# Residual additions of a convolution's output: GpSimd's two additions replaced by four adding transfers

## The chip, the cores and the metric

The kernel runs on one core of one Trainium2 chip. The metric is the device time of one execution in microseconds (us), the median over runs. A core has five engines with instruction streams of their own: TensorE (PE in the profile), which multiplies matrices into PSUM; VectorE (DVE) and ScalarE (ACT), which work elementwise; GpSimd (POOL), and SyncE (SP), which here does nothing but issue transfers (DMA). They meet through semaphores. SBUF is the on-chip memory of 128 partitions.

## The reference

The input is 16 images of 128 channels and 32 x 32 positions, in float32. First comes a self-attention with four heads over the 1024 positions of each image and a residual. Its output, here x1, goes into a quantized residual block:

```python
identity = x
out = act_quant(x)
out = conv3x3(out, weight_quant(w1))
out = batchnorm(out, gamma1, beta1)
out = act_quant(out)
out = conv3x3(out, weight_quant(w2))
out = batchnorm(out, gamma2, beta2)
return out + identity
```

`batchnorm` takes a channel's mean and variance over all images and positions, so nothing of a channel can be normalised before its convolution is done for all 16 images. `act_quant` clips to 0..1 and rounds to 15 steps; the weights are rounded to 7 steps on each side. The last line is the residual addition that this case is about: 16 images of 128 x 1024 numbers.

## The kernel before

**Attention** fills most of the time, up to about 1905 us: TensorE computes scores and weighted sums, ScalarE the exponentials, VectorE combinations of them. In it, sums over blocks of exponentials are kept in tiles `es`: SP sends the first block there (L603), and GpSimd sends the other three with a transfer that adds into the tile (L605, `accum_op`), 189 times in all. The attention's output x1 is stored in DRAM and the first convolution is woven into the attention; its outputs come back from DRAM into tiles `back` (the last image stays in a tile `y`).

**The second convolution** works in three parts by output channels (`LANED`): part 0 has 64 channels, parts 1 and 2 have 32 each. A tile of part 0 puts two images side by side on the 128 partitions, a tile of parts 1 and 2 four images. So part 0 has 8 tiles and parts 1 and 2 have 4 each (`TILES`). For each tile, `convolve` runs nine taps as matmuls for each half of the rows into PSUM (`psd`, L1252); ScalarE copies the result into SBUF (L1263), over an image of the first convolution's output that is no longer needed; VectorE takes statistics of it (BATCH_NORM_STATS2, L1274). In the last tile of a part the statistics are taken from PSUM itself, in three pieces (L1261), after an aggregate of the earlier ones (L1242). `parameters` then makes a scale and a bias out of them (L1237 spreads them over the partitions, L335 to L349 compute), through VectorE and ScalarE in turns. In part 2 a small matmul (`together`, L1312) takes the place of the spreading.

**The order.** Part 0's convolutions come first. Then, for each tile of part 1, TensorE convolves it while two tiles of part 0 are finished; then part 2 is convolved while part 1 is finished; then part 2 is finished with nothing else to do. A scheduler orders each engine's instructions within this; every engine works through its stream in order.

**Finishing a tile** (`finish`): ScalarE scales the tile in place (L1290), an engine adds the residual tile `res` to it in place (L1292), and SP sends it to the output (L1296). The 16 residual tiles (`x1` in the code) have been loaded from DRAM by SP (L1190), each into a tile of its own. The engine is VectorE, but GpSimd for tiles 2 and 5 of part 0 (`BY_POOL`). A GpSimd tile's send is held back and issued behind that of the next VectorE tile. The flag for a general path, which isn't taken here, is written by VectorE after the last addition of part 0 (L1334), and each engine loads it (L1529).

Of the kernel before, what the change touches and what calls it, by code (L numbers as in the profile page):

```python
# [12 lines left out]
ALU = mybir.AluOpType  # L13
# [181 lines left out]
def fast_path(  # L195
# [17 lines left out]
    P = 128  # L213
# [936 lines left out]
    with ExitStack() as ph:  # L1150
# [31 lines left out]
        x1 = {}  # L1182
        laned = lambda v: [v.rearrange("b (c k) n -> k (b c) n", k=step)[lo] for lo, step, _ in LANED]
        x1h, outh = laned(x1d), laned(out)
# [81 lines left out]
        def convolve(part, p):  # L1266
            last = p == TILES[part] - 1
            ends = (0, RPH, H - 8, H) if last else (0, 8, RPH, H) if not part and p == 0 else (0, RPH, H)
            for i, (r0, r1) in enumerate(zip(ends, ends[1:])):
                pair_conv(part, p, r0, r1 - r0, i if last else None)  # L1270
            if not last:
                for hf in range(NHF):
                    with nullcontext() if part else following("DVE"):
                        nc.vector.bn_stats(place2(part, p, hf), results[part, p][:, ts(hf, HALF)])  # L1274
            if p == TILES[part] - 2:
                gather2(part)

        BY_POOL = (2, 5)
        sent = []

        def finish(part, p, scale, bias, ends=(0, N)):
            y = results[part, p]
            for lo, hi in zip(ends, ends[1:]):
                some = y[:, lo:hi]
                if part == 2 and p == 0 and hi <= N // 2:
                    nc.vector.tensor_scalar(some, some, scale, bias, ALU.mult, ALU.add)
                elif len(ends) > 2 and p == 0:
                    nc.scalar.activation(some, some, AF.Identity, bias=bias, scale=scale)
                elif lo == 0:
                    nc.scalar.activation(y, y, AF.Identity, bias=bias, scale=scale)  # L1290
                engine = nc.gpsimd if not part and p in BY_POOL else nc.vector
                added = engine.tensor_tensor(some, some, x1[part, p][:, lo:hi], ALU.add)  # L1292
                sent.append((outh[part][ts(p, P), lo:hi], some))
                if part or p not in BY_POOL:
                    for to, what in reversed(sent):
                        nc.sync.dma_start(out=to, in_=what)  # L1296
                    sent.clear()
            return added

        def parameters(part):  # L1300
            if part < 2:
                spread(part, 0, OWN)
                return bn_params(1, late2[part], gb2[part])
            apart = statp.tile([P, STEPS[part], OWN], F32, name="apart")
            nc.vector.tensor_tensor(
                apart,
                late2[part][:, 0:OWN].unsqueeze(1).to_broadcast([P, STEPS[part], OWN]),
                own_lane.unsqueeze(2).to_broadcast([P, STEPS[part], OWN]),
                ALU.mult,
            )  # L1310
            together = ps_c.tile([P, STEPS[part] * OWN], F32, tag="c", name="together")
            nc.tensor.matmul(  # L1312
                together, lhsT=quad, rhs=apart.rearrange("p s k -> p (s k)"), start=True, stop=True
            )
            return bn_params(1, together, gb2[part])
# [12 lines left out]
        scale2, bias2 = parameters(0)  # L1328
        for p in range(TILES[1]):
            convolve(1, p)  # L1330
            for q in (2 * p, 2 * p + 1):
                added = finish(0, q, scale2, bias2)
        with tc.issue_after(added.ins):
            nc.vector.tensor_copy(flag, worst[0:1, :])  # L1334
        scale2, bias2 = parameters(1)
        for p in range(TILES[2]):
            convolve(2, p)
            finish(1, p, scale2, bias2)
        scale2, bias2 = parameters(2)
        parts = ((0, N // 4, N // 2, N), (0, N // 2, N), (0, N // 2, N), (0, N // 2, N))  # L1340
        for p in range(TILES[2]):
            finish(2, p, scale2, bias2, parts[p])
# [108 lines left out]
def attention_then_quantized_convs(  # L1451
# [50 lines left out]
    def conv_weights(n, wp, behind):  # L1502
# [19 lines left out]

    flag = const.tile([1, 1], mybir.dt.int32, name="flag")
    fast_path(
        nc, tc, x, xturned, wqk, wvo, bo, bnp, x1d, y1d, out, bo_sb, bnp_sb, quad, wq, sc, flag, conv_weights,
        constants,
# [94 lines left out]
```

## Time and profile before

Three runs took 1997.57, 1997.59 and 1999.94 us; the median is 1997.59.

| what | before |
|---|---|
| profiled execution, its own time | 1997.92 us |
| its span, first to last instruction | 1996.1 us |
| TensorE busy | 1975.1 us, 99% of the span |
| VectorE busy | 1528.0 us, 77% |
| ScalarE busy | 1173.3 us, 59% |
| GpSimd busy | 173.4 us, 9% |
| GpSimd's transfers (software_dynamic) | 99.10 MB, 26.2% of the 16 DMA engines' span |
| SP's transfers (hardware_dynamic) | 83.18 MB, 11.0% |

"Busy" is time in instructions; for TensorE their ends are modelled, so it isn't TensorE at its peak. A line of a timeline shows the start, the time, the engine, the kernel's line, the operation, out<-in by the program's names, shapes and the count; in brackets stands the time for which the engine was idle before it and what ended that. The chain that ended last is followed back from the last instruction, at each step to what released it.

### The profile page before, as it was taken

The numbers are of one execution on the slowest core, as the hardware profiler recorded it, in microseconds if no ns is written. First come the engines' busy times: TensorE is split into PE (matmuls) and PEld (weight loads), VectorE is DVE, ScalarE is ACT, GpSimd is POOL, SyncE is SP. The second block draws the span as 40 slices with busy tenths as digits, with TensorE's granted clock in tenths as the row PEclk, the third lists the DMA queues.
The fourth block names the chain that finished last, engine by engine and source line by source line (L and its number), as shares of the span: only waits on it lengthen the run. The fifth ranks groups of instructions, "written<-read, shape, count | busy, mean of one in ns | idle before, by whom it ended". The sixth has DMA issues, their size and how long they took to land.

```text
span 1996.1 us, 27602 instructions
## 1 busy us (share of the span) xinstructions
PE 1975.1 (99%) x10401; PEld 997.9 (50%) x10401; DVE 1528.0 (77%) x2746; ACT 1173.3 (59%) x2028; POOL 173.4 (9%) x215
## 2 busy tenths in 40 slices
PE   9999999999999999999999999999999999999996
PEld 4455544545444454544545454454545445455564
DVE  5886869778687876869777686977868697686887
ACT  4556556565655656555565655655565565556565
POOL 1110010000010010000001001000000100000000
PEclk9999999999999999999999999999999999999998
DMA  4333433334343343334334333343334343333184
GB/s 123 84 86 90 101 68 102 85 85 103 76 102 80 96 95 85 94 67 110 80 95 95 85 95 74 99 91 85 96 86 105 64 105 86 85 93 81 43 332 177
DMA packets 56351, 193.91 MB, mean 97 GB/s; under 512 B 6416, under 2 KB 6800, under 8 KB 56208
## 3 DMA queue, kind: packets, MB, share of 16 engines
q0 software_dynamic: 27216, 99.10, 26.2%
q1 hardware_dynamic: 25872, 83.18, 11.0%
q10 hardware_dynamic: 3120, 9.77, 1.5%
q8 instruction: 83, 1.36, 0.3%
q14 instruction: 60, 0.49, 0.1%
HBM read 35.27 MB, written 24.64 MB: 30 GB/s over the span
## 4 chain that ended last, share of the span: by engine, by line
PE 97%; DVE 2%; ACT 1%; issue 0%; DMA 0%; SPq 0%; DVEq 0%; ACTq 0%
PE pss L413 44%; PE psa L413 38%; PE psu L413 6%; PE pso L413 5%; PE psw L413 2%; PE psd L1252 1%; ACT back L1290 0%; DVE back L1292 0%; DVE early L1274 0%; DMA x<-in_x_dram 0%; PE psv L413 0%; DVE late L1261 0%; ACT steps L1217 0%; PE ps_a L413 0%; ACT rt L338 0%
## 5 line engine op out<-in xcount | busy, mean ns | idle before, releaser
L413 PE MATMUL pss<-u,x 128*64 128x512 f32 (+1 forms) x4128 | 1032.4, 589 | 0.0
L413 PE MATMUL psa<-e,xt 128*64 128x512 f32 x3472 | 897.9, 592 | 0.0
L595 ACT ACTIVATE e<-pss 128x512 f32<-128x512 f32 x1008 | 590.4, 596 | 442.3 <-PE pss L413 436.0
L413 PEld LDWEIGHTS pss<-u,x 128*64 128x64 f32 x4128 | 437.4, 137 | 436.2 <-issue 400.1
L413 PEld LDWEIGHTS psa<-e,xt 128*64 128x64 f32 x3472 | 379.0, 137 | 372.0 <-issue 352.4
L580 DVE TENSOR_TENSOR e<-e 128x512 f32<-128x512 f32 x252 | 171.9, 682 | 298.2 <-ACT e L595 297.8
L581 DVE TENSOR_TENSOR e<-e 128x1024 f32<-128x1024 f32 x252 | 307.6, 1221 | 10.7 <-ACT e L595 9.3
L605 POOL DMA_DIRECT2D es<-e x189 | 163.1, 863 | 1679.2 <-DVE e L584 1401.6
L413 PE MATMUL psu<-x,at_sb 128*64 128x512 f32 x512 | 183.5, 592 | 0.4 <-DMA x<-in_x_dram 0.4
L584 DVE TENSOR_TENSOR e<-e 128x512 f32<-128x512 f32 x252 | 173.0, 686 | 11.3 <-DVE e L581 0.9
L635 ACT COPY ev<-psa 128x512 f32<-128x512 f32 x189 | 99.2, 593 | 63.2 <-PE psa L413 61.8
L413 PE MATMUL pso<-z,wb_sb 128*64 128x512 f32 (+1 forms) x480 | 132.2, 539 | 0.0
L544 ACT ACTIVATE u<-psu,au_sb 128x512 f32<-128x512 f32 x127 | 87.3, 687 | 8.9 <-PE psu L413 6.1
L413 PEld LDWEIGHTS psu<-x,at_sb 128*64 128x64 f32 x512 | 61.2, 137 | 56.1 <-issue 55.5
L671 DVE TRANSPOSE_TENSOR_REDUCE part<-es 128x32 f32<-128x1024 f32 (+1 forms) x65 | 79.4, 1221 | 9.5 <-DMA es<-e 9.5
L711 DVE STREAM_TRANSPOSE rb<-sums 128x1024 f32<-128x1024 f32 (+1 forms) x66 | 79.8, 1210 | 1.6
L731 DVE TENSOR_TENSOR z<-av,rb 128x512 f32<-128x512 f32 x120 | 78.2, 683 | 0.0
L413 PEld LDWEIGHTS pso<-z,wb_sb 128*64 128x64 f32 x480 | 53.1, 137 | 44.5 <-issue 40.8
L802 DVE TENSOR_TENSOR y<-sa,s 64x512 f32<-64x512 f32 x15 | 10.3, 684 | 66.4 <-ACT sa L786 66.4
L1252 PE MATMUL psd<-padf,wq 128*32 128x512 bf16 (+3 forms) x792 | 60.0, 358 | 0.4 <-DVE padf L1204 0.4
L661 ACT COPY ev<-y 64x512 f32<-64x512 f32 x63 | 38.8, 616 | 33.2 <-DVE y L658 32.0
L413 PE MATMUL psw<-rows,filters 128*64 128x256 bf16 x540 | 57.5, 277 | 0.0
(199 smaller groups left out, 1354.4 us busy)
## 6 DMA issues: line engine op xcount, KB each, us to landing
es<-e POOLq DMA_DIRECT2D x189, 512.0 KB, 4.5
es<-e SPq DMA_DIRECT2D x63, 512.0 KB, 2.9
xt<-in_xturned_dram SPq DMA_DIRECT2D x32, 256.0 KB, 3.1
x_dram<-acc SPq DMA_DIRECT2D x16, 512.0 KB, 2.9
res<-x_dram SPq DMA_DIRECT2D x16, 512.0 KB, 10.3
x<-in_x_dram ACTq DMA_DIRECT2D x15, 512.0 KB, 3.9
y_dram<-y SPq DMA_DIRECT2D x15, 512.0 KB, 2.6
out_dram<-back SPq DMA_DIRECT2D x12, 512.0 KB, 3.7
```

Of the source, the lines that this page charges most:

```text
L413: done = nc.tensor.matmul(out_, lhsT=lhsT, rhs=rhs, start=start, stop=stop)
L544: copied = nc.scalar.activation(dst, ps, AF.Identity, bias=au_sb[:, h : h + 1])
L580: nc.vector.tensor_tensor(e[:, T3], e[:, B12], e[:, B22], ALU.add)
L581: nc.vector.tensor_tensor(e[:, T1 : T2 + 1 : T2 - T1], e[:, B12 : B11 + 1], e[:, B11 : T3 + 1 : T3 - B11], ALU.subtract)
L584: return nc.vector.tensor_tensor(e[:, T4], e[:, T2], e[:, B21], ALU.add)
L595: exps[:] = [nc.scalar.activation(e[:, 2 * c + 1 - m], ps, AF.Exp).ins]
L605: nc.gpsimd.dma_start(out=sides[g], in_=mine, accum_op=ALU.add)
L635: nc.scalar.copy(evs[g][i], psa[g][i])
L671: nc.vector.tensor_reduce(part, total.rearrange("p (k c) -> p k c", c=Q), AX.X, ALU.add, apply_transpose=True,)
L711: nc.vector.transpose(rb, rinv.unsqueeze(2).to_broadcast([P, n, Q]))
L731: nc.vector.tensor_tensor(z[:, 2 * (h % 2) + 1 - m], av[:, ts(m, HALF)], rb[:, ts(m, HALF)], ALU.mult)
L1252: nc.tensor.matmul(ps[lane], lhsT=wq[1][:, tap, LANED[part][2]], rhs=pads2[STEPS[part] * p + i][:, r0 + dy : r0 + dy + n_rows, dx : dx + W ...
```

## The change

In part 0, tiles 1, 3, 5 and 7 are no longer added by an engine. Once ScalarE has scaled such a tile, GpSimd issues a transfer from it that adds into the residual's tile, and SP sends the residual's tile to the output. VectorE adds tiles 0, 2, 4 and 6; GpSimd adds none itself. The sends of the adding tiles wait in a list: each is issued by SP behind the send of the next VectorE tile of part 0, and the last one ahead of whatever part 1 sends first. In the compiled order SP sends tiles 0, 2, 1, 4, 3, 6, 5, 7 of part 0 (before: 0, 1, 3, 2, 4, 6, 5, 7), then loads the flag, then sends part 1's.

```diff
-        BY_POOL = (2, 5)
-        sent = []
+        BY_DMA = [(0, p) for p in (1, 3, 5, 7)]
+        waiting, added = [], []
 
         def finish(part, p, scale, bias, ends=(0, N)):
...
-                engine = nc.gpsimd if not part and p in BY_POOL else nc.vector
-                added = engine.tensor_tensor(some, some, x1[part, p][:, lo:hi], ALU.add)
-                sent.append((outh[part][ts(p, P), lo:hi], some))
-                if part or p not in BY_POOL:
-                    for to, what in reversed(sent):
-                        nc.sync.dma_start(out=to, in_=what)
-                    sent.clear()
-            return added
+                to = outh[part][ts(p, P), lo:hi]
+                if (part, p) in BY_DMA:
+                    nc.gpsimd.dma_start(out=x1[part, p], in_=y, accum_op=ALU.add)
+                    waiting.append((to, x1[part, p]))
+                    continue
+                added[:] = [nc.vector.tensor_tensor(some, some, x1[part, p][:, lo:hi], ALU.add)]
+                sends = [(to, some)]
+                sends = waiting + sends if part else sends + waiting
+                waiting.clear()
+                for to, what in sends:
+                    nc.sync.dma_start(out=to, in_=what)
...
             for q in (2 * p, 2 * p + 1):
-                added = finish(0, q, scale2, bias2)
-        with tc.issue_after(added.ins):
+                finish(0, q, scale2, bias2)
+        with tc.issue_after(added[0].ins):
```

## The prediction

> **What bounds the kernel now.** I read the page's engine totals first. They name TensorE at 99% of a span of 1996.1 us, but that is an average, and the edit touches only the second convolution's output stage, from about 1948 us on. So I asked for the timelines of the engines there. VectorE, from the first residual addition (columns: start, us, engine, line, operation, out<-in, shape, count):
>
> ```profile
> 1949.32 1.22 DVE L1292 TENSOR_TENSOR back<-back,res 128x1024 f32<-128x1024 f32 x1 [1.31 <-ACT back L1290]
> ...
> 1953.68 2.45 DVE L1292 TENSOR_TENSOR back<-back,res 128x1024 f32<-128x1024 f32 x1 [0.81 <-ACT back L1290]
> 1956.06 0.68 DVE L1274 BATCH_NORM_STATS2 early<-back 128x6 f32<-128x512 f32 x1
> 1956.66 3.30 DVE L1292 TENSOR_TENSOR back<-back,res 128x1024 f32<-128x1024 f32 x1
> ...
> 1960.49 2.34 DVE L1292 TENSOR_TENSOR back<-back,res 128x1024 f32<-128x1024 f32 x2
> ```
>
> One addition takes 1.22 us, but two take 2.45 and 3.30. GpSimd's timeline shows what runs beside those two:
>
> ```profile
> 1952.66 2.39 POOL L1292 TENSOR_TENSOR back<-back,res 128x1024 f32<-128x1024 f32 x1 [42.40 <-ACT back L1290]
> 1956.48 2.40 POOL L1292 TENSOR_TENSOR back<-back,res 128x1024 f32<-128x1024 f32 x1 [1.43 <-ACT back L1290]
> ```
>
> GpSimd's additions end at 1955.05 and 1958.88; VectorE's end at 1956.13 and 1959.96, 1.08 after each. VectorE stood still while GpSimd added: 2.45 - 1.22 + 3.30 - 1.22 = 3.3 us lost. Then the chain that ended last, from 1960 to 1981:
>
> ```profile
> 1960.56 2.26 DVE back L1292 x2
> ...
> 1964.61 1.28 DVE late L1261 x3
> ...
> 1976.07 2.39 DVE early L1274 x4
> ...
> 1978.99 1.28 DVE late L1261 x3
> ```
>
> It is VectorE's without a wait for TensorE: part 1's last statistics end at 1965.89, part 2's at 1980.27. TensorE's timeline says when they could have been made:
>
> ```profile
> 1964.82 12.18 PE L1252 MATMUL psd<-padf,wq 128*32 128x512 bf16 x252
> 1980.76 0.42 PE L1312 MATMUL together<-apart,quad 128*128 128x84 f32 x2 [3.77 <-DVE apart L1305]
> ```
>
> The last convolution ends at 1976.99 (1980.76 - 3.77), and TensorE has run without a gap since 1934.68. The images that part 2 reads first (tile pad) are read again from 1960.85, so part 1's convolution ends about 1961.05. VectorE is late by 4.4 us after part 1 (1965.9 against 1961.05 and one 0.43 us statistic) and by 2.8 us after part 2. After that comes a tail with no convolution in it: parameters, the last additions, stores.
>
> **What the skill says.** The Trainium skill's "SBUF — State Buffer", section "Who interferes with whom", says that a VectorE instruction with two SBUF inputs and a GpSimd instruction that reads SBUF exclude each other. The trace agrees: 2.45 and 3.30 us instead of 1.22. The same section infers that such a VectorE addition doesn't collide with the writing of transfer descriptors by GpSimd. The trace agrees again: the attention phase issues 189 adding transfers from GpSimd (L605), among 252 VectorE additions of L581, which took 1180 to 1228 ns. "DMA: Bandwidth & Descriptors", section "SWDGE vs HWDGE vs iDMA", says that adding during a transfer is possible from GpSimd's queue alone; the trace has these, in just this size and type:
>
> ```profile
> L605 POOL DMA_DIRECT2D es<-e x189: 852/859/1172, 21.4 to 1866.9; - x189
> DMA to landing us min/median/max: 4.5/4.5/6.6
> ```
>
> **The change part by part.** The compiled order of the changed kernel has TensorE's and ScalarE's streams as before; VectorE loses two additions, GpSimd swaps two additions for four transfers, SP's sends change order and waits.
>
> 1. *GpSimd's two additions go* (tiles 2 and 5). Their 4.8 us were on GpSimd, off the chain; what they gave VectorE's chain is the 3.3 us above.
> 2. *VectorE does tiles 0, 2, 4, 6 instead of 0, 1, 3, 4, 6, 7*: two fewer, 1.14 us each back to back (1949.32 to 1950.46), so 2.3 us. With the first item VectorE has 5.6 us less work before part 1's statistics.
> 3. *Who is late next there?* ScalarE. It scales the eight tiles and empties part 1's PSUM without an idle moment from 1948.04 to 1960.10 (its last two copies start at 1959.03 and take 1.07), and waits there neither for GpSimd nor for the additions. VectorE then goes: addition 4 when ScalarE has tile 4 (1955.2), statistics (1956.9), addition 6 when it has tile 6 (1957.95, ends 1959.1), statistics of tile (1,2)'s halves 1959.6 and 1960.2, ending 1960.8. Before, the same statistic ended at 1964.09 and the aggregate with the last three followed in 1.80 us (1965.89). So part 1's end comes at 1962.6: **3.3 us earlier**, not 5.6; the other 2.3 become waits for ScalarE. TensorE's 1961.05 isn't the limit.
> 4. *Part 2*. From part 1's end to part 2's VectorE alone needs 1980.27 - 1965.89 = 14.38 us, so it would end at 1977.0. But the last statistic waits for the last convolution: 1976.99 + 0.02 + 0.43 = **1977.44**. Gain at this point: 1980.27 - 1977.44 = **2.8 us**; TensorE has become the bound, by about 0.45 us.
> 5. *The tail*, 1980.27 to 1996.1 = 15.8 us, has the same instructions and is taken as unchanged.
> 6. *Four transfers by GpSimd*: 0.86 us of its queue each; it has nothing else to do. Cost if that were not hidden from VectorE: 4 x 0.86 = 3.4 us; bound below, nothing (no L581 addition stretched). I take 0.
> 7. *Landing*. ScalarE has tiles 1, 3, 5, 7 at 1950.9, 1953.65, 1956.4, 1959.15. With 0.9 for issue and 4.5 to land the last is there at about 1964.6. Load: GpSimd's queue had 26.2% of the 16 engines for 189 transfers, 0.262 x 1996 / 189 = 2.8 us each; SP's queue from 1945 to 1997 had 44.5% of 52 us for 17.4 transfers of 512 KB, 1.33 us each. Four and eight of them make 21.7 us; started at 1951, all are through by 1972.7 even if none overlapped a pause. So landing lies between 1963.6 (at once) and 1972.7; I take 1965.
> 8. *SP's queue*. Sends of tiles 1, 3, 5, 7 now wait for those landings. Behind them in SP's order stand the sends of 4, 6, the load of the flag, and part 1's sends, the first of which is ready at 1972.10 - 3.3 = 1968.8. Last landing at 1965: nothing is held. At 1972.7: part 1's sends go some 4 us late, still ahead of part 2's first (1984.60 - 2.8 = 1981.8), on which the end depends. Cost 0; cover 16 us.
> 9. *Waits elsewhere*: the residual tiles, now destinations, aren't used again; ScalarE's copies into the neighbouring images got no new wait. Nothing.
>
> Sum: -2.8 us. The profiled execution took 1997.92 us, 1.8 around its span and 0.3 above the median. Its span becomes 1993.3; the median 1997.59 - 2.8 = **1994.8 us**, 0.14% less. A difference of 0.2% (4.0 us) is about what a measurement of this kernel can tell from no change, so this counts as the same.
>
> **Rivals.** *Part of the gain is lost* (ScalarE, or VectorE in part 2, is later than I have it). For: the margin over TensorE is only 0.45 us, and my new order of some ten VectorE instructions was laid out by hand. Each us of lateness beyond the margin costs one: 0.5 to 2 us lost, 1995.3 to 1996.8. *Hidden anyway*: the tail, not the statistics, sets the end (the last stores' landing). Against it: the chain passes through every statistic and the last send (1990.1) follows VectorE's last addition by 0.9 us. It gives 1997.6. *Slower*: head of line on SP. If the adding transfers crawl under the competing stores, tile 7's send, with part 1's and part 2's behind it, holds the last store. It begins to cost when tile 7 lands after about 1979.7 (five sends of 0.4 us before 1981.8), and makes the kernel slower by 0.2% when it lands 2.8 + 4 us later, 27 us after issue. Against: 4.5 median, 6.6 longest of 189. It would give 2002 or more. *More than 4 us faster* needs the tail to shorten as well; TensorE forbids it before that. GpSimd not adding through the transfer is excluded by the compiled order; so is an unaltered VectorE.
>
> **How the numbers follow.** TensorE becomes the bound, 1994.8 (1994.2 to 1995.4): 0.57. Partly lost: 0.13. Hidden, or up to 0.2% slower for a stall I don't see: 0.08. Slower by over 0.2%, head of line or anything of its size: 0.15. Faster by over 4.0 us: 0.07. So faster 0.08 (with the edge of the first case), same 0.77, slower 0.15. The range holds the first two and the hidden case, 1993.4 to 1998.6; the likeliest alone 1994.2 to 1995.4.
>
> **What would show it.** GpSimd: no addition, four transfers of 0.86 us. VectorE: four additions of about 1.2 us at L1296, none stretched; part 1's last statistics ending near 1962.6, before which VectorE idles for ScalarE's scalings. The chain between 1969 and 1977.4 should return to TensorE's convolutions, and the last statistic (L1261) should wait for them. SP: part 1's sends from 1969. I am wrong if a VectorE addition stays above 2 us, if the last landing is after 1980, or if the tail from the last statistic isn't about 15.8 us.

## The result, and the profile after

The changed kernel took 1994.66 us (median of 22 runs, 1993.83 to 1996.13) against 1997.87 for the kernel before, measured beside it. The ratio is 0.9985 with a 95% interval of 0.9978 to 0.9991. The interval leaves out 1, so the change gains some 3 us. That is less than the 0.2% (4.0 us) which the prediction named as what a measurement of this kernel can tell from no change; with 22 runs of each it can tell this much too. The profiled execution took 1994.76 us with a span of 1993.0.

In this execution the part that wasn't changed ran 0.7 us earlier. Over the ten kernels profiled here that part ends anywhere from 1947.36 to 1948.54, so this is taken as chance. Times below are counted from the start of part 0's first scaling by ScalarE (L1290), 1948.04 in the kernel before and 1947.36 after:

| us after the first scaling | before | predicted | after |
|---|---|---|---|
| part 1's last statistic ends | 17.85 | 14.6 | 14.70 |
| part 2's last statistic ends | 32.23 | 29.4 | 29.36 |
| end of the span | 48.06 | 45.2 | 45.64 |

The lines that answer to those of before: VectorE's timeline of the changed kernel has four additions (now L1296), all of one length, with a wait for ScalarE in front of each (before, two of the six in part 0 had one):

```profile
1948.64 1.22 DVE L1296 TENSOR_TENSOR back<-back,res 128x1024 f32<-128x1024 f32 x1 [1.31 <-ACT back L1290]
...
1951.87 1.22 DVE L1296 TENSOR_TENSOR back<-back,res 128x1024 f32<-128x1024 f32 x1 [0.45 <-ACT back L1290]
...
1954.61 1.23 DVE L1296 TENSOR_TENSOR back<-back,res 128x1024 f32<-128x1024 f32 x1 [0.45 <-ACT back L1290]
...
1957.36 1.23 DVE L1296 TENSOR_TENSOR back<-back,res 128x1024 f32<-128x1024 f32 x1 [0.45 <-ACT back L1290]
...
1960.71 1.35 DVE L1261 BATCH_NORM_STATS2 late<-psd 128x6 f32<-128x512 f32 x3
...
1976.29 0.43 DVE L1261 BATCH_NORM_STATS2 late<-psd 128x6 f32<-128x256 f32 x1 [0.19 <-PE psd L1252]
```

Nothing is stretched, and the last line has what the kernel before lacked: VectorE waits for TensorE. The chain that ended last, from 1944 us on, says the same in its first pieces:

```profile
1943.99 32.27 PE psd L1252 x543
...
1976.29 0.44 DVE late L1261
```

Where before VectorE and ScalarE stood from 1945 to 1980, one piece of TensorE's convolutions now runs through. GpSimd's timeline and the summary of its transfers (last line):

```profile
1950.76 0.87 POOL L1293 DMA_DIRECT2D res<-back  x1 [41.01 <-ACT back L1263]
...
1958.76 0.86 POOL L1293 DMA_DIRECT2D res<-back  x1 [1.89 <-DVE flag L1337]
```

```profile
L1293 POOL DMA_DIRECT2D res<-back x4: 859/859/874, 1950.8 to 1958.8; - x4
DMA to landing us min/median/max: 5.2/8.9/10.8
```

The issue costs 0.86 us as in the attention, but landing, the time from issue until the transfer is reported complete, takes up to 10.8 us against 4.5 (median) there.

### The profile page after: what moved, and what is told of

It is laid out like the page before. It is cut to its first block, busy times and chain, and to the rows that moved or that the text cites. A ratio compares the mean times of both kernels' runs of the same rounds, so it can differ in the third digit from the quotient of the medians.

```text
span 1993.0 us, 27598 instructions
## 1 busy us (share of the span) xinstructions
PE 1974.7 (99%) x10401; PEld 991.4 (50%) x10401; DVE 1523.2 (76%) x2744; ACT 1173.4 (59%) x2028; POOL 172.7 (9%) x217
## 4 chain that ended last, share of the span: by engine, by line
PE 98%; DVE 1%; ACT 0%; issue 0%; DVEq 0%; POOL 0%; ACTq 0%; POOLq 0%
PE pss L413 44%; PE psa L413 39%; PE psu L413 6%; PE pso L413 5%; PE psd L1252 3%; PE psw L413 2%; PE unread L413 0%; PE psv L413 0%; PE ps_a L413 0%; DVE steps L1219 0%; DVE back L1296 0%; PE psr L413 0%; ACT steps L1217 0%; DVE pad L1222 0%; DVE late L292 0%
## 5 line engine op out<-in xcount | busy, mean ns | idle before, releaser
L581 DVE TENSOR_TENSOR e<-e 128x1024 f32<-128x1024 f32 x252 | 307.7, 1221 | 10.7 <-ACT e L595 9.2
L605 POOL DMA_DIRECT2D es<-e x189 | 163.0, 863 | 1669.4 <-DVE e L584 1403.7
```

The costliest lines, as they stand in the source:

```text
L581: nc.vector.tensor_tensor(e[:, T1 : T2 + 1 : T2 - T1], e[:, B12 : B11 + 1], e[:, B11 : T3 + 1 : T3 - B11], ALU.subtract)
L605: nc.gpsimd.dma_start(out=sides[g], in_=mine, accum_op=ALU.add)
```

## The experiments

The theory: VectorE's two long additions stood still for GpSimd's; without that, ScalarE bounds part 1 and TensorE part 2; the transfers are hidden. The rivals: it is the number of VectorE's additions that counts; VectorE is still the bound; the transfers cost the end something. All were profiled and timed, in 13 or 21 runs each, beside the kernel before (median 1997.79 and 1997.49 us in the two series). Their numbers together:

| kernel | part 1 | part 2 | end of span | median us | ratio to before (95%) |
|---|---|---|---|---|---|
| before | 17.85 | 32.23 | 48.06 | 1997.87 | |
| changed, 4 transfers | 14.70 | 29.36 | 45.64 | 1994.66 | 0.9985 (0.9978 to 0.9991) |
| 2 transfers (tiles 2, 5) | 15.41 | 29.78 | 45.5 | 1995.28 | 0.9987 (0.9981 to 0.9994) |
| none, VectorE adds 8 | 15.87 | 30.24 | 45.6 | 1995.84 | 0.9990 (0.9982 to 0.9998) |
| GpSimd adds 4 | 16.20 | 30.57 | 46.7 | 1996.00 | 0.9991 (0.9982 to 0.9999) |
| no addition in part 0 | 14.69 | 29.43 | 45.5 | 1995.24 | 0.9989 (0.9982 to 0.9995) |
| 6 transfers | 14.70 | 29.43 | 45.3 | 1994.77 | 0.9986 (0.9979 to 0.9993) |
| 8 transfers | 14.69 | 29.36 | 49.9 | 2000.49 | 1.0015 (1.0008 to 1.0021) |
| 8, sent by GpSimd | 14.69 | 29.38 | 51.3 | 2000.96 | 1.0016 (1.0009 to 1.0023) |
| changed, two late stores by ScalarE | 14.70 | 29.38 | 45.1 | 1995.12 | 0.9988 (0.9982 to 0.9995) |

"Part 1" and "part 2" are the ends of the last statistics, from the first scaling, in the profile. The ratios' intervals reach 0.06 to 0.08% (1.3 to 1.6 us) to either side, so single medians here can't order neighbours; for parts 1 and 2 the stage times of the profiles can, as they agree within 0.1 us in the six kernels that have the same bounds.

**Two transfers.** Tiles 2 and 5, GpSimd's before, go by transfers; VectorE keeps its six additions.

```diff
-        BY_DMA = [(0, p) for p in (1, 3, 5, 7)]
+        BY_DMA = [(0, p) for p in (2, 5)]
```

> The changed kernel with tiles 2 and 5 alone added by transfers (those that GpSimd added before); VectorE keeps its six additions of part 0. Times are counted from the start of part 0's first scaling by ScalarE: in the kernel before, part 1's last statistic ends 17.9 us after it and part 2's 32.2; in the changed kernel 14.7 and 29.4. Theory (GpSimd's additions held VectorE up for 3.3 us, and TensorE is the bound now): no VectorE addition above 1.3 us; part 1's end at 15.2, since VectorE adds tile 7 after ScalarE has it; part 2's at 29.4 to 29.7; 2.5 us faster than before, at most 0.4 slower than the changed kernel. Rival (the number of VectorE's additions counts, and their stretching was not GpSimd's doing): additions still above 2 us, part 1's end near 17.9, no faster than before.

VectorE's six additions in part 0 are all 1.2 us, two of them among these lines of its timeline:

```profile
1953.12 1.23 DVE L1296 TENSOR_TENSOR back<-back,res 128x1024 f32<-128x1024 f32 x1 [0.81 <-ACT back L1290]
1954.26 0.69 DVE L1274 BATCH_NORM_STATS2 early<-back 128x6 f32<-128x512 f32 x1
1954.87 1.21 DVE L1296 TENSOR_TENSOR back<-back,res 128x1024 f32<-128x1024 f32 x1
```

In the kernel before, the same two took 2.45 and 3.30. With the same number of VectorE's additions as before, 2.45 of the 2.87 us at part 2's end are there. The rival that only the number counts falls. The ends are 0.2 and 0.1 us later than expected, and part 2's is not TensorE's here: VectorE's last three statistics (from 1975.91, 1.35 us) run without a wait. So the last 0.4 us of the changed kernel's gain do come from its having two additions fewer.

**None.** VectorE adds all eight.

```diff
-        BY_DMA = [(0, p) for p in (1, 3, 5, 7)]
+        BY_DMA = []
```

> The changed kernel with no transfer and no GpSimd: VectorE adds all eight tiles of part 0. Theory (two more additions of 1.14 us cost less than the 3.3 us of standing still): all additions 1.2 us, part 1's end at 16.8 us after the first scaling, part 2's at 31.2, VectorE without a wait for TensorE there; 1.0 us faster than before. Rival (only fewer VectorE additions help): part 1's end at 20.1 and 2.3 us slower than before.

Two more additions on VectorE and yet faster than before: 15.87 at part 1's end, 2.0 us earlier, where I expected 1.0. The sum had left out that the kernel before waits 0.81 us for ScalarE in front of its third addition; with two more additions VectorE is never that early, and the wait is filled. Two additions back to back, with no wait before them, show it:

```profile
1952.60 2.34 DVE L1296 TENSOR_TENSOR back<-back,res 128x1024 f32<-128x1024 f32 x2
```

From the first addition to the end of part 1's ordinary statistics VectorE works without a pause: 8 x 1.14 + 6 x 0.61 = 12.8 us.

**GpSimd adds four.** The transfers of the changed kernel become GpSimd's additions, everything else stays.

```diff
-                    nc.gpsimd.dma_start(out=x1[part, p], in_=y, accum_op=ALU.add)
+                    nc.gpsimd.tensor_tensor(x1[part, p], x1[part, p], y, ALU.add)
```

> The changed kernel with its four transfers replaced by GpSimd's additions of tiles 1, 3, 5, 7 into the residual's tiles; SP's order of sends is the same, and so are VectorE's four additions. Theory (exclusion): VectorE's additions of tiles 2, 4, 6 wait for GpSimd, 1.8 to 2.9 us each, part 1's end at 16.4 us after the first scaling, part 2's at 30.8; 1.5 us faster than before, 1.3 slower than the changed kernel. Rival (only the number of VectorE's additions counts): additions of 1.2 us, 14.7 and 29.4, the time of the changed kernel.

VectorE's three later additions, in its timeline, and GpSimd's four in its own:

```profile
1952.52 1.98 DVE L1296 TENSOR_TENSOR back<-back,res 128x1024 f32<-128x1024 f32 x1 [0.45 <-ACT back L1290]
...
1955.27 2.56 DVE L1296 TENSOR_TENSOR back<-back,res 128x1024 f32<-128x1024 f32 x1 [0.17 <-ACT back L1290]
...
1958.35 2.81 DVE L1296 TENSOR_TENSOR back<-back,res 128x1024 f32<-128x1024 f32 x1
```

```profile
1951.02 2.40 POOL L1293 TENSOR_TENSOR res<-res,back 128x1024 f32<-128x1024 f32 x1 [40.71 <-ACT back L1290]
1953.70 9.69 POOL L1293 TENSOR_TENSOR res<-res,back 128x1024 f32<-128x1024 f32 x3 [0.28 <-ACT back L1290]
```

The first GpSimd addition ends at 1953.42, VectorE's beside it at 1954.50, again 1.08 later, and the next two pairs end 1.08 and 1.09 apart. It works both ways: the three GpSimd additions that VectorE's run beside take 3.05, 3.37 and 3.35 us, not 2.4. So one engine stands while the other adds, here with 1.5 us lost at part 1's end against the transfers (16.20 and 14.70; 16.4 expected).

**No addition in part 0.**

```diff
+                if not part:
+                    nc.sync.dma_start(out=to, in_=some)
+                    continue
                 if (part, p) in BY_DMA:
...
-        with tc.issue_after(added[0].ins):
+        with tc.issue_after(added[0].ins) if added else nullcontext():
```

> The changed kernel without any residual addition in part 0: ScalarE scales the eight tiles and SP sends them as they are (the residual of these 64 channels is left out); no transfer from GpSimd. It says what the additions of part 0 still cost. Theory (TensorE is the bound and the four transfers are hidden): part 1's last statistic ends 14.7 us and part 2's 29.4 us after part 0's first scaling, the changed kernel's values; time within 0.5 us of the changed kernel, some 3 us below the one before. Rival (the four transfers cost the tail something by their load): the same 29.4, but the end 0.7 us or more earlier than in the changed kernel.

The second place is needed as VectorE has no addition in part 0 behind which the flag could be written; it is the same in the two kernels with eight transfers below. Without any work for the residual in part 0 the statistics end where they end with four transfers (14.69 and 29.43), and the end of the span, 45.5, is the changed kernel's within 0.2. That is the floor: nothing that shows is left to gain from the additions of part 0, as TensorE bounds part 2:

```profile
1977.54 0.43 DVE L1261 BATCH_NORM_STATS2 late<-psd 128x6 f32<-128x256 f32 x1 [0.28 <-PE psd L1252]
```

The median (1995.24) is 0.6 above the changed kernel's, within what these medians can tell.

**Eight and six transfers.**

```diff
-        BY_DMA = [(0, p) for p in (1, 3, 5, 7)]
+        BY_DMA = [(0, p) for p in range(8)]
...
```

> All eight tiles of part 0 are added by transfers, none by VectorE. Theory: part 1's end at 14.6 and part 2's at 29.4 us after the first scaling, as in the changed kernel, since ScalarE and then TensorE are the bounds, so nothing is gained at the last statistic. The transfers are 33 us of work of all 16 engines (8 of 2.8 and 8 stores of 1.33), from about 2 us after the first scaling, so the last lands 30 to 34 us after it; part 1's sends stand behind it on SP and run into part 2's, and the end comes 0.5 to 4 us later than in the changed kernel. Rival 1 (transfers stay hidden): the changed kernel's time within 0.3 us. Rival 2 (VectorE was still the bound): 2 us or more faster than the changed kernel.

The statistics didn't move by a tenth, so VectorE isn't the bound. But the kernel became slower than the one before, by 2.7 us, and than the changed one by 5.8. SP's row of the waits says on what its sends stood, and the summary how long the landings took:

```profile
SPq L1301 <- DMA res<-back: 38.9, 8, 15.1
```

```profile
DMA to landing us min/median/max: 4.6/12.8/21.7
```

The last landing (the send behind it starts at 1981.07) came 33.1 us after the first scaling, as worked out; the price was higher than I had put it, 0.5 to 4 us: 4.3 us at the end of the span and 5.8 in the medians. Six transfers (`(1, 2, 3, 5, 6, 7)` in the same line):

> Six transfers (tiles 1, 2, 3, 5, 6, 7); VectorE adds tiles 0 and 4. With all eight by transfers the last landing came 33.1 us after the first scaling and the end 4.3 us late; with four, 22.2 us and nothing. Here 6 x 2.8 + 8 x 1.33 = 27.4 us of work from about 2 us on. Theory (a landing after some 31.7 us begins to cost, as then the sends behind it reach the last part's): last landing at 26 to 29, statistics at 14.7 and 29.4, the end 0 to 1 us later than in the changed kernel. Rival (each transfer beyond four costs its share, 1 us or more): 2 us or more later.

The last landing came 26.7 us after the first scaling and the end was not later than with four.

**Eight, sent by GpSimd.** Is the loss with eight due to SP's sends standing behind the landings? Here all eight tiles are added by transfers again, and GpSimd itself sends them:

```diff
...
-                sends = [(to, some)]
-                sends = waiting + sends if part else sends + waiting
+                for late, what in waiting:
+                    nc.gpsimd.dma_start(out=late, in_=what)
                 waiting.clear()
-                for to, what in sends:
-                    nc.sync.dma_start(out=to, in_=what)
+                nc.sync.dma_start(out=to, in_=some)
...
```

> All eight tiles of part 0 by transfers, and their sends issued by GpSimd behind the eight, so that nothing of SP's waits for a landing. The work of the DMA engines is that of the kernel with all eight sent by SP. Theory (head of line: SP's 13 later sends, held until the last landing and then issued at 0.8 us each, made that kernel's end 4.3 us late): the end is back within 1 us of the changed kernel, part 1's sends go at some 20 us after the first scaling. Rival (load: the 16 engines have too much work before the end, whoever issues it): the end stays 3 us or more late, with the last stores landing late.

My theory fell. SP's sends of part 1 now went from 1968.63 on, 20.9 us after the first scaling and held by nothing, and the end was not earlier but 1.4 us later (51.3 against 49.9). What stayed is the load. Stretches of four kernels (columns: window, length, then busy time of PE, PEld, DVE, ACT, POOL, TensorE's clock, the share of time in which the DMA engines were busy, and GB/s), first the changed one, then the one with six, then all eight sent by SP, then all eight sent by GpSimd:

```profile
1974.00:1981.00 7.00, 2.65 (x78) 1.97 (x70) 5.61 (x19) 2.63 (x6) 0.00 (x0) 0.98 0.53 208
```

```profile
1974.00:1981.00 7.00, 2.75 (x82) 2.28 (x72) 5.54 (x19) 2.54 (x6) 0.00 (x0) 0.98 1.00 395
```

```profile
1950.00:1971.00 21.00, 21.00 (x424) 10.51 (x420) 12.47 (x29) 16.68 (x22) 6.62 (x8) 1.00 0.99 226
1974.00:1981.00 7.00, 3.24 (x90) 2.26 (x82) 5.60 (x18) 2.04 (x5) 0.00 (x0) 1.00 1.04 296
```

```profile
1950.00:1971.00 21.00, 21.00 (x424) 11.74 (x420) 12.46 (x29) 16.65 (x22) 9.62 (x14) 1.00 1.01 187
1974.00:1981.00 7.00, 3.05 (x86) 2.47 (x78) 5.60 (x18) 2.24 (x5) 0.53 (x1) 1.00 1.03 401
```

With four transfers the DMA engines have a pause before the tail; with six and with eight they are busy in that stretch throughout, but with six the additions are through by then and only stores run (395 GB/s). Where mostly adding transfers run they move 187 GB/s, where stores run 401: 512 KB take 2.8 us of all engines when added and 1.3 when stored. Eight additions and the 8 MB of output are 8 x 2.8 + 16 x 1.3 = 43 us of work from about 2 us after the first scaling, so by this estimate the last store can't have moved before 45, and the changed kernel's span ends at 45.6 with landing and closing included. With six the work is 38 us, with four 32, which leaves room. SP's last two sends took longer to issue, too, in the kernel with eight sent by GpSimd: 2.54 us together (SP's timeline), against 1.28 in the changed kernel and with eight sent by SP.

```profile
1990.07 2.54 SPq L1300 DMA_DIRECT2D out_dram<-y  x2
```

So the load is enough to explain the loss. The trace of the kernel with eight sent by SP also bounds what SP's hold, its sends standing behind the landings, can have added there. From 1949 to 1997.9 the DMA engines were busy for 91.2% of the time, which is 44.6 us of work. It began at about 1951, so without any pause it would end at about 1995.6; the last store had moved by 1995.4. The one dip between, with a share of 0.83, is from 1981 to 1983, just behind the last landing. By this estimate the hold cost some 0.3 us, of a loss of 4.3.

**Two late stores by ScalarE's queue.** In the changed kernel SP's last send starts at 1986.89, 1.2 us after VectorE's last addition ends (1985.67), behind other sends.

```diff
+                other = (part, p, lo) in ((2, 2, N // 2), (2, 3, 0))
                 for to, what in sends:
-                    nc.sync.dma_start(out=to, in_=what)
+                    (nc.scalar if other else nc.sync).dma_start(out=to, in_=what)
```

> The changed kernel with two of the last part's stores (the second half of its third tile, the first half of its last) issued by ScalarE's queue, idle by then, and not by SP's, whose last send starts 1.1 us after VectorE's last addition. Theory (SP's issuing, 0.4 to 0.6 us a send, is late at the very end): the last send starts within 0.2 us of the last addition; 1.0 us faster than the changed kernel, 4 us than the one before. Rival (the stores' landing on loaded engines sets the end): no difference to the changed kernel.

The last send did start 0.06 us after the last addition (1985.85, 1985.91), and the span's end came 0.5 us earlier (45.1). That is half of the 1.0 us expected, and no more than the tails of the kernels without it differ by (15.3 to 16.3 us from part 2's end). The median shows nothing of it: 1995.12 against 1994.66. A gain of 1 us is not excluded, nor shown. No version beat the changed kernel by more than the measurement can tell.

## Why the prediction was right

*The bound before.* The 3.3 us of standing still beside GpSimd is shown by two kernels: gone with GpSimd's additions (two transfers), larger in sum with four of them. In the kernel before, VectorE's additions ended 1.08 us behind GpSimd's; with four GpSimd additions the three pairs have 1.08 to 1.09. Most of the gain is this: two transfers alone give 2.45 of the 2.87 us.

*Steps 1 to 3, part 1's end.* 14.70 against 14.6 worked out. ScalarE is the bound there, as said: with no VectorE additions at all it stays 14.69.

*Step 4, part 2's end.* 29.36 against 29.40; the cap by TensorE is shown by the kernels with six transfers, with eight, and without any addition in part 0, which leave VectorE less work and have the same end (29.36 to 29.43). The gain at this point is 2.87 us, forecast 2.8. The order of five kernels at this point (changed 29.4, two transfers 29.8, none 30.2, GpSimd's four 30.6, before 32.2) is that of their medians.

*Step 5, the tail.* 16.3 us in the profile of the changed kernel, against 15.8 before. Up to the end of VectorE's last addition it is the same 8.95 us in both; the difference lies behind it, in the stores (7.3 against 6.9 us). In the other kernels with up to six transfers the tail was 15.3 to 16.1, without an order by their transfers. With one profile of each, why it varies by half a microsecond either way stays open; it is more than I allowed for.

*Step 6.* No addition of the changed kernel took more than 1.23 us, but none of them ran beside one of its four issues, so it doesn't test the step; the statistics that did run beside issues kept their 0.69 us. The test is in the attention: there 14 of the 252 additions of L581 ran beside an issue of L605, for 0.5 us each, and took 1.22 to 1.23 us.

*Step 7, the landing,* was the term I mis-sized. I took 17 us after the first scaling (1965) for the last one; its send went at 22.2. Between the two ends that I had given, the load (24.7) was the better guide than the landing of a single transfer in the attention (4.5 us), as stores ran beside.

*Step 8, SP.* Therefore part 1's first send was held: its addition ended at 1968.24, the send started at 1970.94, 2.7 us late. Tile 7's send went ahead of it at 1969.54, and the load of the flag lies between the two. As written there, a hold of this size cost nothing.

*The sum* was right by its pieces and in part by luck. The profiled span became 3.1 us shorter: 0.7 from the part that wasn't changed, 2.9 at part 2's end, less 0.45 in the tail; the first and the last are not in the sum and nearly cancel. The median fell by 3.2 us, where 2.8 was forecast, from a start that lies 0.3 above the median of three runs I had. So 1994.66 against 1994.8 is closer than the working earns; the gain is known no better than to 1.3 us either way.

*The rival on the slower side* had the wrong mechanism. Slower by transfers is possible and was seen, with eight. But it came with the load of the DMA engines: with SP's sends freed the end was as late. The landing was only just past the point that I had named (33.1 against 31.7 us), where 1.4 us would have been the price by my reckoning, and not the 4.3 of the span or the 5.8 of the medians.

## What to carry to other kernels

Before moving work to an idle engine, look at whether the busy engine's instructions grow beside it: here two GpSimd additions took 3.3 us from VectorE, and giving them back to VectorE would have been faster already. Then ask who is late next: of the 5.6 us taken off VectorE, 2.4 went to waits for ScalarE (part 1 ends 3.15 us earlier) and 0.3 to one for TensorE (part 2, 2.87), and removing the additions altogether gained no more than moving half of them. An adding transfer is hidden only as long as the DMA engines get through all their work, the stores included, before the last stores are due; count its time on all of them, about twice a store's, and not only its landing. Six fitted here, eight did not.

## What the runs showed that I had not expected

- The engines' throughput with adding transfers is half of that with stores (187 against 401 GB/s at a share of 1.0), and landings grow with the load: 4.5 us (median) in the attention, up to 10.8 with four, 15.3 with six, 21.7 with eight in flight beside their stores.
- Issuing one store on SP's queue took anything from 0.33 to 1.7 us already in the kernel before (median 0.38, L1296), so that a queue of sends is itself late; with eight transfers the median for the sends of parts 1 and 2 was 0.64. What sets it within a run stays open.
- With six transfers the DMA engines have no pause from 1974 to 1981 either (a share of 1.00, at 395 GB/s), and the end is not later than with four. Busy DMA engines are no loss by themselves; what counts is whether their work is through in time.
